# Four graph layers on one TensorE queue: another order of steps for the first and the last graphs, stored as data

## The chip, the cores and the metric

The kernel runs on one core of a Trainium2 chip. The metric is the device time of one launch in microseconds. Before the change three runs took 2764.44, 2767.73 and 2769.32 us; the median is 2767.73 us. A fourth run was taken with the hardware profiler.

## What is computed

Thirty-two graphs of 512 nodes with 256 features each pass through four layers; each layer ends in a residual and a layer norm. All is float32, and no graph needs another one.

```python
# per graph: x is 512x256, adj is 512x512
x = layernorm(x + relu(((1 + eps) * x + adj @ x) @ W1 + b1) @ W2 + b2)      # layer 0
x = layernorm(x + attention_4_heads(x, adj > 0.5, W, a_src, a_dst) + bias)  # layer 1
x = layernorm(x + attention_8_heads(x, log(adj + 1e-6), Wq, Wk, Wv) @ Wo.T + bo)  # layer 2
x = layernorm(x + softmax(((x @ W3) @ x.T) * adj) @ x)                      # layer 3
```

## The kernel before

**A list of steps, and an order.** The program does not emit its instructions graph by graph. `prepare()` and `graph(g)` register small steps in a `Plan`: each has a name, an engine, an assumed duration, the steps that it must follow, and the buffers that it takes and frees. `Plan.run` (L222) then puts all 11,118 steps of all graphs in one sequence and emits them in it; every engine executes its own part strictly in that order. I call the weight preparation set 0 and the graphs 1 to 32, so "28.d1" is the step d1 of graph 28. The order mixes the stages of several graphs: while one graph is in layer 3, the next ones are in layers 2, 1 and 0.

**How the order was found.** `Plan.order` (L134) walks forward with assumed times. Among the steps that could start soon it takes the one with the earliest due time: the graph's turn times a period of 83.965, less the longest remaining chain behind the step, plus a correction by step name, with further corrections for the first graphs, for the last graphs and for single graphs. These numbers are in one line of 78,550 characters at L1609.

**Steps that matter here** (TensorE steps, with the chain that each waits for):

- `d1` (L1175) sums the layer-1 weights. It waits for `as` (L1165), eight VectorE additions that may begin when the head's matmul `o1` (L1137) has read the weights.
- `o100` to `o111` (L1137) wait for `zm` (VectorE, L1115), these for `z` (ScalarE, L1104), and these for `Rl` (L1052), a 1 MB load that spreads a row over all partitions. It comes out of `Rt` (L1035) through a small store.
- `n0` to `n7` (L1351) wait for `m` (VectorE, L1315), these for `e` (ScalarE, L1306), these for the scores `s0` to `s7` (L1293).
- `i0`, `i1` (products recorded at L342 or L346, out iT_ps) open layer 3. In graphs 3 to 29 they wait for a turned copy of x: after `p1` come a residual and norm statistics on VectorE, one small step on GpSimd, `r3` on ScalarE, a 512 KB store to DRAM `xw3` (L710), four 128 KB loads `xl3` (L723) and two VectorE transposes `xe3` (L742).
- `la` (L821) loads a graph's adjacency in four pieces of 256 KB, `lx` (L833) its x. VectorE turns the adjacency (`at`), then `h0`, `h1` start the graph.
- `cd` and `fd` (GpSimd, L1326 and L1379) start DMAs that add one layer-2 weight tile to another.

SyncE issues `la`, `lx`, `Rl`, `xw3`, `xl3` and the outputs in one queue[...].

**Three forms of matmul.** A product is one matmul of 128 columns or, after a column-tiled step, four of 32 columns side by side (`product`, L342 and L346): such a step takes the form that TensorE is in. The scores `s` always use row tiles, `d2` tiles of 64 rows. `Plan.CHANGE` (L64) charges 0.14 to 0.22 for a change of form.

Of the kernel before, what the change touches and what calls it, by code (L numbers as in the profile page):

```python
# [16 lines left out]
P = 128  # L17
# [19 lines left out]

class Step:
# [4 lines left out]
    def __init__(self, eng, us, after, take, mode, emit):  # L43
        self.eng, self.us, self.after, self.take, self.emit = eng, us, after, take, emit
        self.mode = mode
        self.then, self.frees = [], []


class Plan:
# [51 lines left out]
    def link(self):  # L101

        self.left = [{} for _ in self.steps]
        for g in reversed(range(len(self.steps))):
            steps, left = self.steps[g], self.left[g]
            for name, s in steps.items():
                for a in s.after:
                    (self.steps[0][a[1:]] if a[0] == "^" else steps[a]).then.append((g, name))
            for k, (_, after) in enumerate(self.frees[g]):
                for a in after:  # L110
                    steps[a].frees.append(k)
        for g in reversed(range(len(self.steps))):
            steps, left = self.steps[g], self.left[g]
            for name in reversed(steps):
                s = steps[name]
                left[name] = s.us + max(
                    (self.left[h][n] + self.hop(s, self.steps[h][n]) for h, n in s.then if h - g < 2),
                    default=0.0,
                )
# [6 lines left out]
    def ready(self, g, name, ends):  # L126

        s, t = self.steps[g][name], 0.0
        for a in s.after:
            h, n = (0, a[1:]) if a[0] == "^" else (g, a)  # L130
            t = max(t, ends[h][n] + self.hop(self.steps[h][n], s))
        return t

    def order(self, period, ahead, window, stay, rush=(), moves=(), edges=(0, (), 0, (), ())):  # L134


        room = {b: [(0.0, i) for i in range(n)] for b, n in self.stock.items()}
        engine, mode, out, last = {}, "", [], 0.0
        held = [{} for _ in self.steps]
        ends = [{} for _ in self.steps]  # L140
        waits = [{n: len(s.after) for n, s in steps.items()} for steps in self.steps]
        fwaits = [[len(after) for _, after in frees] for frees in self.frees]
        ready, low, opened = {}, 0, 0
        todo = [len(steps) for steps in self.steps]
        moved = dict.fromkeys((n for steps in self.steps for n in steps), 0.0)
        turn = [max(g - 1, 0) for g in range(len(self.steps))]
        for i, early in enumerate(rush):
            turn[-1 - i] -= early
        for n, far in moves:
            moved[n] += far  # L150
        lead, tail = edges[0], len(self.steps) - edges[2]
        early, late = dict(edges[1]), dict(edges[3])
        own = {g % len(self.steps): dict(far) for g, far in edges[4]}

        def shift(g, name):
            some = early if g <= lead else late if g >= tail else {}
            return moved[name] + some.get(name, 0.0) + own.get(g, {}).get(name, 0.0)

        def near(low):
            fill, until, between, left, drain = ahead  # L160
            return fill if low < until else drain if low >= len(self.steps) - left else between

        def open_to(n):
            nonlocal opened
            while opened < min(n, len(self.steps)):
                for name in self.steps[opened]:
                    if not waits[opened][name]:
                        ready[opened, name] = self.ready(opened, name, ends)
                opened += 1

        open_to(window)
        while low < len(self.steps):
            found = []
            for (g, name), t in ready.items():
                s = self.steps[g][name]
                t = max(t, engine.get(s.eng, 0.0))
                into = self.EITHER.get(mode, "c32") if s.mode == "any" else s.mode
                change = self.CHANGE[into] if s.eng == "pe" and into != mode else 0.0
                for k, (kind, _, rest) in enumerate(s.take):
                    r, n = room[kind], sum(b[0] == kind for b in s.take[:k])  # L180
                    if len(r) <= rest + n:
                        break
                    t = max(t, r[n][0])
                else:
                    due = turn[g] * period - self.left[g][name] + shift(g, name) + stay * change
                    found.append((t, due, g, name, change))
            if not found:
                return math.inf, out
            first = min(found)[0] + near(low)
            _, t, g, name, change = min((due, t, *f) for t, due, *f in found if t <= first)  # L190
            s = self.steps[g][name]
            t += change
            if s.eng == "pe":
                mode = self.EITHER.get(mode, "c32") if s.mode == "any" else s.mode
            del ready[g, name]
            got = {}
            for kind, key, _ in s.take:
                got[key] = held[g][key] = (kind, room[kind].pop(0)[1])
            if s.eng:
                engine[s.eng] = t + s.us  # L200
            end = ends[g][name] = t + s.us
            last = max(last, end)
            out.append((g, name, mode, got))
            for h, n in s.then:
                waits[h][n] -= 1
                if not waits[h][n] and h < opened:
                    ready[h, n] = self.ready(h, n, ends)
            for k in s.frees:
                fwaits[g][k] -= 1
                if not fwaits[g][k]:  # L210
                    key, after = self.frees[g][k]
                    kind, i = held[g].pop(key)
                    free = max(ends[g][a] + self.HOP.get(self.steps[g][a].eng, 0.0) for a in after)
                    room[kind].append((free, i))
                    room[kind].sort()
            todo[g] -= 1
            while low < len(self.steps) and not todo[low]:
                low += 1
                open_to(low + window)
        return last, out  # L220

    def run(self, tries):  # L222

        self.link()
        best = min((self.order(*t)[0], t) for t in tries)
        assert best[0] < math.inf
        for g, name, self.mode, got in self.order(*best[1])[1]:
            self.slot[g].update((key, i) for key, (_, i) in got.items())
            self.steps[g][name].emit()
# [3 lines left out]
def fast_path(  # L233
# [24 lines left out]
    B, N, D = x.shape  # L258
# [27 lines left out]
    selfw = const.tile([P, P], F32, name="selfw")  # L286
# [21 lines left out]
    def blk(i):  # L308
# [3 lines left out]
    plan = Plan({  # L312
        "B": 13, "C": 12, "D": 10, "p": 8,

        "live": 6, "L0": 1, "L1": 2, "L2": 2, "L3": 1, "AT": 4, "zs": 7, "edge": 1, "tmp": 2,
    })
# [1737 lines left out]
@with_exitstack  # L2054
def four_layer_graph_kernel(ctx: ExitStack, tc: tile.TileContext, *args):
    flags = ctx.enter_context(tc.tile_pool(name="flags", bufs=1))
    beyond = flags.tile([1, 1], I32, name="beyond")
    fast_path(tc, *args, beyond)
    taken = tc.nc.values_load(beyond, min_val=0, max_val=1,
                              skip_runtime_bounds_check_because="is_lt gives 0 or 1")  # L2060
    with tc.If(taken > 0):
        general_path(tc, *args)
# [34 lines left out]
```

## Time and profile before

| | |
|---|---|
| median of three runs | 2767.73 us |
| the profiled execution | 2767.12 us, of it the span 2765.3 us |
| share of the span: TensorE, VectorE, ScalarE, GpSimd | 98%, 78%, 62%, 17% |
| mean granted TensorE clock | 0.994 |
| DMA, mean over the span | 151 GB/s |
| one graph in the middle: from 1297.05 to 1380.02, from the matmul group y_ps of one graph to that of the next | 82.97 us |
| the last group of matmuls of the last graph ends at | 2752.6 us |

Thirty-two times 82.97 us is 2655.0 us; the other 110.3 us of the span are the preparation, the filling of the pipeline and its emptying. In the groups below, "idle before" a matmul is time in which TensorE had nothing that it could do, and the arrow names what ended it. A matmul's end is modelled in the profile, so some waiting may lie inside the busy time too.

### The profile page before, as it was taken

Reading aid. Unit: us, or ns where it says so; the run is one execution under the profiler, and the core shown is the slowest. Engines: PE = TensorE matmul, PEld = TensorE weight load, DVE = VectorE, ACT = ScalarE, POOL = GpSimd, SP = SyncE. Lnnn points to the kernel's source line nnn. Section 1 sums busy time; section 2 is a strip of 40 time slices with the busy share of each in tenths; the row PEclk is TensorE's granted clock in tenths of the full one; section 3 lists DMA queues with packets and bytes.
Section 4 is the critical chain, followed back from the end, with each engine's and each line's share of the span. In section 5 each row is a group of like instructions: output and inputs, shape, how many; then the busy total and the mean of one; then the engine's idle time right before and its main releaser. Section 6 shows DMA issues by size and latency. Waiting matters only on the chain.

```text
span 2765.3 us, 68089 instructions
## 1 busy us (share of the span) xinstructions
PE 2716.7 (98%) x28680; PEld 1317.9 (48%) x28680; DVE 2158.8 (78%) x4257; ACT 1720.4 (62%) x3320; POOL 474.8 (17%) x526
## 2 busy tenths in 40 slices
PE   8999999999999999999999999999999999899998
PEld 6544444444445444445444445444444443444443
DVE  3887778877879877879877879877878877578975
ACT  3676665666666666666666666666665665556853
POOL 1111211121111121111121111121111111111110
PEclk9999999999999999999999999999999999999999
DMA  8487787778888879888878888888896988736760
GB/s 167 80 168 150 148 168 147 160 160 163 158 163 151 171 157 169 162 156 153 174 162 160 149 171 151 171 157 169 155 163 135 182 168 163 156 73 146 155 131 17
DMA packets 476735, 418.76 MB, mean 151 GB/s; under 512 B 377788, under 2 KB 431496, under 8 KB 444552
## 3 DMA queue, kind: packets, MB, share of 16 engines
q0 software_dynamic: 45568, 277.89, 53.1%
q1 hardware_dynamic: 429872, 136.18, 24.2%
q8 instruction: 227, 3.72, 0.5%
q14 instruction: 84, 0.69, 0.1%
q10 hardware_dynamic: 984, 0.28, 0.0%
HBM read 155.53 MB, written 31.24 MB: 68 GB/s over the span
## 4 chain that ended last, share of the span: by engine, by line
PE 86%; DVE 6%; DMA 3%; issue 2%; ACT 1%; POOL 0%; SPq 0%; DVEq 0%; POOLq 0%; ACTq 0%
PE s L1293 8%; PE o_ps L1351 7%; PE v_ps L346 7%; PE y_ps L342 7%; PE o_ps L346 6%; PE o_ps L1137 6%; PE hT_ps L346 6%; PE s L346 5%; PE h1T_ps L346 4%; PE o2p_ps L346 3%; PE iT_ps L342 3%; PE s L342 3%; PE h1T_ps L342 3%; PE kT_ps L342 2%; DVE z L1115 2%; PE qT_ps L346 2%
## 5 line engine op out<-in xcount | busy, mean ns | idle before, releaser
L1315 DVE SCALAR_TENSOR_TENSOR z<-AT,z 128x1024 f32<-128x1024 f32 x512 | 612.6, 1214 | 108.2 <-ACT z L1306 107.0
L1306 ACT ACTIVATE z<-s 128x512 f32<-128x512 f32 x1024 | 541.4, 608 | 109.2 <-PE s L1293 103.4
L1104 ACT ACTIVATE z<-R_bc,nT,S 128x512 f32<-128x512 f32 x512 | 373.4, 807 | 72.0 <-DMA z<-z 58.2
L684 ACT ACTIVATE x<-x,shift,rstd 128x256 f32<-128x256 f32 x508 | 273.9, 593 | 179.6 <-DVE shift L669 174.8
L1115 DVE SCALAR_TENSOR_TENSOR z<-z,T,edge 128x512 f32<-128x512 f32 x512 | 346.5, 742 | 5.8 <-ACT z L1104 5.8
L1326 POOL DMA_DIRECT2D z<-z x186 | 174.4, 942 | 868.4 <-PE o_ps L1351 445.3
L661 POOL TENSOR_TENSOR rstd<-ve,nhalf 128x4 f32<-128x4 f32 (+1 forms) x131 | 169.0, 1339 | 854.8 <-DVE ve L655 846.6
L1293 PE MATMUL s<-qT,kT 32*128 32x512 f32 x2048 | 278.4, 626 | 0.4 <-ACT kT L1264 0.4
L1351 PE MATMUL o_ps<-z,v 128*32 128x512 f32 x2048 | 254.9, 599 | 2.6 <-DVE z L1315 1.4
L1539 DVE TENSOR_TENSOR z<-s,AT 128x512 f32<-128x512 f32 x128 | 88.4, 690 | 214.9 <-PE s L342 110.1
L1137 PE MATMUL o_ps<-z,v 128*32 128x512 f32 x2048 | 233.8, 595 | 2.5 <-DVE z L1115 2.5
L1165 DVE TENSOR_TENSOR z<-z 128x1024 f32<-128x1024 f32 (+1 forms) x256 | 229.5, 949 | 0.7 <-PE o_ps L1137 0.7
L638 DVE BATCH_NORM_STATS2 st<-x 128x6 f32<-128x256 f32 x508 | 212.7, 419 | 10.6
L346 PE MATMUL o_ps<-x,z 128*32 128x257 f32 x3520 | 202.4, 380 | 0.0
L346 PE MATMUL hT_ps<-AT,x 128*32 128x256 f32 (+2 forms) x2640 | 185.5, 380 | 0.0
L342 PE MATMUL y_ps<-w_sb,h1T 128*128 128x256 f32 x832 | 184.4, 379 | 0.0
L342 PEld LDWEIGHTS y_ps<-w_sb,h1T 128*128 128x128 f32 x832 | 156.1, 190 | 21.5 <-issue 1.0
L1293 PEld LDWEIGHTS s<-qT,kT 32*128 32x128 f32 x2048 | 96.7, 184 | 143.5 <-issue 63.6
L346 PEld LDWEIGHTS o_ps<-x,z 128*32 128x32 f32 x3520 | 114.8, 110 | 83.8 <-issue 6.9
L346 PE MATMUL h1T_ps<-hT,w_sb 128*32 128x512 f32 x1296 | 147.9, 595 | 0.0
L625 POOL DMA_DIRECT2D x<-biases x96 | 103.8, 1081 | 237.0 <-issue 67.7
L346 PE MATMUL s<-iT,xT 128*32 128x512 f32 x1232 | 139.4, 592 | 0.1
(188 smaller groups left out, 3858.7 us busy)
## 6 DMA issues: line engine op xcount, KB each, us to landing
z<-z POOLq DMA_DIRECT2D x186, 1024.0 KB, 8.7
x<-biases POOLq DMA_DIRECT2D x96, 512.0 KB, 9.6
R_bc<-R_dram SPq DMA_DIRECT2D x32, 1024.0 KB
Ar<-in_adj_dram SPq DMA_DIRECT2D x124, 256.0 KB
z<-z POOLq DMA_DIRECT2D x62, 512.0 KB, 7.7
x<-in_x_dram SPq DMA_DIRECT2D x32, 512.0 KB
out_dram<-x SPq DMA_DIRECT2D x31, 512.0 KB
x_dram<-x SPq DMA_DIRECT2D x27, 512.0 KB
```

Source lines behind the costliest of these rows:

```text
L342: nc.tensor.matmul(out, lhsT, rhs, start=start, stop=stop)
L346: nc.tensor.matmul(out[part], lhsT[:, part], rhs, start=start, stop=stop)
L638: nc.vector.bn_stats(t[f"st{n}"][:, c, :], t["xo" if n == 4 else "x"][:, c, :D])
L684: nc.scalar.activation(t[into][:, c, :D] if into else xn, xn, AF.Identity, bias=t[f"shift{n}"][:, c : c + 1], scale=t[f"rstd{n}"][:, c : c ...
L1104: nc.scalar.activation(t[f"e{h}"][:, c, :], t["Rbc"][:, h, :], AF.Relu, bias=t["nT"][:, h, c : c + 1], scale=t["S"][:, h, c : c + 1],)
L1115: nc.vector.scalar_tensor_tensor(z, z, t["T"][:, h, c : c + 1], t["edge"][:, c, :], op0=ALU.add, op1=ALU.mult)
L1137: nc.tensor.matmul(po[32 * q : 32 * q + 32, :], t["v"][:, c, hp * P + 32 * q : hp * P + 32 * q + 32], t[f"e{2*hp+q//2}"][:, c, :], start=( ...
L1165: nc.vector.tensor_add(z[:, :m, :], z[:, :m, :], z[:, m : 2 * m, :])
L1293: nc.tensor.matmul(pk, t["k"][hs, o, blk(c)], t["q"][hs, o, :], start=True, stop=True)
L1306: nc.scalar.activation(t[f"E{k}"][:, j, :], t[f"ps{k}{j}"], AF.Exp, scale=QSCALE)
L1315: nc.vector.scalar_tensor_tensor(z, t["AT"][:, c, None, :].to_broadcast([P, 2, N]), ADJ_EPS, z, op0=ALU.add, op1=ALU.mult,)
L1351: nc.tensor.matmul(t[f"n{o}"][32 * j : 32 * j + 32, :], t["v2"][:, c, o * P + F2 * j : o * P + F2 * (j + 1)], t[f"E{k}"][:, j, :], start=( ...
```

## The change

The search is gone from the kernel. The order is a constant string: two bytes for each step, namely how far its graph lies ahead of the oldest unfinished one, and its place among that graph's steps that are left. `sequence` unpacks it, and `run` walks it once with the old assumed durations, only to decide which buffer of a kind each step gets.

```diff
+ORDER = (
+    'c-rk;*^=bA4Fo}ux~uw{@%D}<?En8tBNL#idcEV=h<$Q|)H78&cp-6+Dx@SLCAZiUY;jy-Po=2(Kg9|4bIQx=--7b0qlKcZttiWH'
...
+)
-    def order(self, period, ahead, window, stay, rush=(), moves=(), edges=(0, (), 0, (), ())):
...
-            first = min(found)[0] + near(low)
-            _, t, g, name, change = min((due, t, *f) for t, due, *f in found if t <= first)
...
+    def sequence(self, text):
+        data = zlib.decompress(base64.b85decode(text))
+        left, low = [list(steps) for steps in self.steps], 0
+        for ahead, place in zip(data[: len(data) // 2], data[len(data) // 2 :]):
+            g = low + ahead
+            yield g, left[g].pop(place)
+            while low < len(left) and not left[low]:
+                low += 1
+        assert low == len(left)
-    def run(self, tries):
+    def run(self, text):
         self.link()
...
+        for g, name in self.sequence(text):
...
+            s.emit()
...
     with tc.manual_schedule():
...
+        plan.run(ORDER)
```

No step is added, removed or altered: both programs have the same 11,118 steps with the same instructions but for the form that a product takes. Of TensorE's 2,077 steps, the 1,317 from t1 of graph 4 to h1 of graph 28 stand at the same places in both; about 360 before and 400 after them stand in another order. On the other engines the same holds: VectorE keeps 2,076 of 3,242 steps in one unchanged stretch, ScalarE 2,025 of 3,193, GpSimd 331 of 509, SyncE 309 of 467.

TensorE's order near the end, as an example (a step's form: ' column tiles, r row tiles, R rows by 64):

```
before: 28.o100' 29.h1' 28.o101' 28.o110' 28.o111' 27.s6r 28.yt0 28.yt1 28.yt2 28.yt3 28.d1' 29.f0'
after:  28.o100' 28.o101' 28.o110' 29.f0' 29.f1' 29.f2' 28.o111' 29.f3' 28.d1' 27.n6' 28.dt 28.yt0

before: 27.p1' 29.y0' 29.y1' 28.s5r 30.h0' 28.s6r 30.h1' 28.n5' 28.s7r 28.n6' 29.xt10 29.xt11
        30.f0 30.f1 28.n7' 29.v10' 29.v11' 29.v12' 29.v13' 27.i0'
after:  27.p1' 28.s6r 28.n3' 28.n4' 29.y1' 28.n5' 28.s7r 30.h0' 30.h1' 28.n6' 30.f0' 29.xt10 29.xt11
        30.f1 29.v10 29.v11 29.v12 29.v13 30.f2 29.Rt 30.f3 27.i0
```

and SyncE's there:

```
before: 30.la0..3 30.lx 25.out 31.la0 31.lx 31.la1..3 27.xw3 26.out 27.xl30..33 29.Rs 29.xs 29.hsb 29.Rl
        32.la0 32.lx 32.la1..3 28.xw3 28.xl30..33 27.out
after:  25.out 30.la0..3 30.lx 31.la0..2 27.xw3 27.xl30..33 31.la3 31.lx 29.xs 29.Rs 29.Rl 29.hsb 26.out
        28.xw3 32.la0..2 28.xl30..33 32.la3 30.Rs 30.Rl 32.lx
```

## The prediction

> **What bounds the kernel now.** I read first the page's shares and its 40 slices.
>
> ```profile
> PE 2716.7 (98%) x28680; PEld 1317.9 (48%) x28680; DVE 2158.8 (78%) x4257; ACT 1720.4 (62%) x3320; POOL 474.8 (17%) x526
> ...
> PE   8999999999999999999999999999999999899998
> ```
>
> TensorE (PE) is the bound: full in all slices but the first, one late one and the last. An order without fewer matmuls can win only what TensorE does not use. So I cut the span into stretches of 83 us, about one graph each, by the windows view (columns: stretch, its length, busy time of PE, PEld, DVE, ACT and POOL, granted clock, DMA share, GB/s).
>
> ```profile
> 249.00:332.00 83.00, 81.19 (x773) 38.35 (x769) 59.70 (x103) 51.82 (x106) 15.22 (x17) 1.00 0.77 142
> ...
> 498.00:581.00 83.00, 83.00 (x925) 40.15 (x921) 67.77 (x134) 53.40 (x105) 14.89 (x16) 1.00 0.80 155
> ...
> 2240.00:2323.00 83.00, 79.55 (x804) 36.16 (x797) 63.55 (x122) 50.57 (x97) 13.70 (x15) 0.98 0.82 162
> 2323.00:2406.00 83.00, 74.94 (x849) 35.52 (x848) 46.89 (x92) 39.36 (x80) 12.57 (x15) 0.96 0.89 176
> ...
> 2489.00:2572.00 83.00, 79.42 (x836) 39.26 (x830) 72.27 (x148) 55.95 (x104) 11.72 (x13) 0.98 0.62 134
> ```
>
> The middle has no hole, and there both programs have one order: nothing is to be won or lost there. The holes lie before 500 us and after 2100 us, where the order changes. The wait view, cut to these two parts, names them (engine, line, what it waited for: total, times, longest): first from 2100 us on, then from 12 to 500 us.
>
> ```profile
> PE iT_ps L346 <- DVE xT L742: 8.0, 1, 8.0
> PE d_ps L1175 <- DVE z L1165: 3.4, 2, 3.1
> ...
> PE o_ps L1137 <- DVE z L1115: 2.5, 2, 1.5
> PE o_ps L1351 <- DVE z L1315: 1.4, 1, 1.4
> ```
> ```profile
> PE d_ps L1175 <- DVE z L1165: 2.3, 2, 1.7
> PE gg L546 <- DVE gm L540: 2.0, 1, 2.0
> PE o_ps L1351 <- DVE y L1210: 1.3, 1, 1.3
> ```
>
> With the smaller ones the waits sum to 8.1 us in the first part and 20.0 in the last, leaving out the final check's. A wait costs more than itself: behind some the granted clock drops.
>
> ```profile
> 2386.90:2390.30 3.40, 3.34 (x17) 0.68 (x18) 0.60 (x2) 0.64 (x4) 0.00 (x0) 0.54 0.95 193
> ...
> 2513.00:2516.40 3.40, 3.40 (x34) 1.53 (x28) 3.39 (x6) 3.40 (x7) 0.93 (x1) 0.52 0.78 140
> ...
> 2646.00:2649.40 3.40, 3.40 (x16) 0.70 (x12) 2.60 (x7) 1.40 (x3) 2.75 (x3) 0.50 1.15 231
> ```
>
> In 3.4 us at half clock half the work is done: 1.7 us lost. It happens five times (near 212, 2294, 2383, 2513, 2646), once with only 3.0 us of it under matmuls: about 8.3 us. Here a rule speaks against this reckoning. The Trainium skill, "TensorE: Matmul & The Clock Gate", section "Why this matters for your kernels", has the clock fall only after a gap of some 3 us. By it only the 8.0 us wait would cost, 1.5 us. The trace has the drop behind 1.26 us (at 211.69), 1.38 and 1.49 us, yet none behind 1.70 us at 259.59. I follow the trace: a removed wait of over 1.2 us takes 1.7 us along where the trace shows it.
>
> **The change, part by part.** For every TensorE step I looked up its latest TensorE ancestor and summed the matmul work that stands between the two in each order (h 3.5, f 1.77, y 3.46, o1 1.74, i, p, w, q and k 1.72, v 0.89, n and s 0.86, d1 1.0: intervals between starts in the middle of the trace). That cover must outlast the other engines' chain.
>
> *d1 of graph 28* waited 3.05 us, to 2294.89. Its eight additions cost 4 times 1.22 and 4 times 0.68, 7.6 us of VectorE; the cover from o110 was 3.7 us. After: 8.8. The wait goes, with the clock: 4.7 us. *d1 of graphs 4 and 5* waited 1.70 and 0.64; cover 7.0 becomes 18.3 and 9.6: 2.3 us. Graphs 27, 29 and 30 get 7.0, a length at which 0.1 to 1.7 us were waited: 0.5 each goes into the new stalls below.
>
> *i0 of graph 27* is the largest: 7.96 and 1.5. Its cover hardly moves, 27.8 to 27.7. What decides is the chain behind 27.p1 (end at 2350.8), which the chain view shows (start, us, what):
>
> ```profile
> 2361.71 0.57 SPq L723
> 2362.33 1.42 SPq L723
> 2363.80 4.56 SPq L723
> 2368.40 5.02 DMA xL<-x_dram
> ...
> 2374.54 11.47 issue
> 2386.10 0.72 DVE xT L742
> 2386.96 3.41 PE iT_ps L346 x16
> ```
>
> The turned loads started 10.9 us after p1; VectorE then waited until 2386.0. In the semaphore records 15 of 16 parts of the last load are in by 2379.1 and the last one at 2385.9. Before them in the queue stood 27.xw3 and 26.out, 512 KB each, and behind 2326 us five loads for graph 31. After: 26.out stands behind, and 31.la3 and 31.lx too; 31.la0 to la2 stand directly ahead. They need graph 30's adjacency turned; after the change that lies about 15 us of matmul work before 27.p1, so they are likely issued before xw3 is ready. Without 26.out (2.4 us between the landings of xw3 and it) and without a late part: 28.3 - 2.4 + 1.6 for xe3 = 27.5 us against 27.7: no wait. If parts come late again: 7 us. In graph 28 the whole chain took 29.2 us, a wait of 1.5. I take 3.5 with its clock, so 6 of 9.5 are won; the ends are 0 and 9.5.
>
> *o100, o101 of graph 30* waited 1.49 and 1.00, with a drop. Cover from Rt 24.2 and 29.4 becomes 26.9 and 32.1, 2.7 more than before, and the waits sum to 2.5. Taken 3.5 of 4.2. *n4 of graph 2* (1.26 and a drop): cover 3.5 becomes 21.1, 3.0 us. *dt of 32 and n4 of 31* (0.49, 1.38, a drop): n6 no longer follows so closely, n4 has 13.8 for 12.0 and dt 1.3 for 0.1, but VectorE is behind there with the additions of graph 32 in both orders; taken 2.0 of 3.6. *k0* followed its copy directly in graphs 2, 5, 27 and nearly in 6, and waited 0.24, 0.24, 0.24, 0.66; s0 of graph 2 0.45: cover grows in all of them, 1.8.
>
> *The start.* SyncE issues x second, and the third and fourth adjacency pieces wait for other landings; both orders need all 1.5 MB and the fourth piece before h0, and that one waits for the load of a0 in both. On ScalarE three small bias loads now stand between the first and the second copy of the adjacency. In the trace their last one was held until 8.1 us by another load. After, it waits for the third adjacency piece, which lands earlier (issued without a wait). I take nothing, with 2 us either way. gg of the preparation (2.0) has less cover, 0.4 for 1.4, but VectorE no longer has graph 2's adjacency between: 1.0 won. Against that f0 of graph 1 follows its copies directly (0.3), and Rt of graph 1 stands 0.3 behind v13, where 1.3 of cover and 0.2 of waiting were seen: 1.2 lost. Sum -0.5.
>
> *Changes of form.* Two s steps in a row take 1.93 us, one alone 1.07: entering row form costs 0.21, and by a fit over 1,200 groups entering the full form 0.06 and column form from the full one 0.02. Counted over both orders, entries to row form fall from 187 to 179, to the full form from 135 to 120, to column form by 18: 1.7 + 0.9 + 0.4 = 3.0 us. The planner's 0.14 to 0.22 for each would say 7; the trace decides.
>
> *The end.* Behind the last matmul (2752.6) the same steps follow. SyncE now issues the outputs of 31, 30 and 29 together just before those of 32: 1.5 MB in the 10.5 us before 32's first, 143 GB/s, with the DMA otherwise idle (the last slice has 17 GB/s). Nothing, at most 2 us.
>
> Sum: 4.7 + 2.3 + 6 + 3.5 + 3.0 + 2.0 + 1.8 - 0.5 + 3.0 = 25.8. Against it I set 2.8 for stalls that the old trace cannot show: the three d1 at 7.0 (1.5) and three s0 at 1.1 us behind their copies, where 1.9 was seen without a wait (1.3). Net 23: the profiled execution's 2767.1 becomes 2744.1; its time lies 0.6 below the median of the runs, so from 2767.7 I say 2744.7.
>
> **Rivals.** *The waits move (0.22).* VectorE is busy 72 of 83 us near 2500; a gap that one step leaves is taken by the next. If 27.i0 keeps its 9.5 us and the three d1 wait 1.7 each with one drop, 25.8 - 6 - 5.3 - 2 leaves 12: 2756. For it: i0's cover has not grown. Against it: the other covers grow well beyond the waits. *All goes (0.15).* Every wait of 28.1 us, the drops of 8.3 and the 3.0 would give 2728 at most; more likely 2733. *No change (0.10):* new waits of some 20 us, as much as the old ones. *Slower (0.08).* SyncE's queue in order: 32.la0 to la2 now stand between 28.xw3 and 28.xl3, 31.la0 to la2 before 27.xw3, 32.la3 before 30.Rl. In the old trace SyncE needed from 2326.06 to 2342.94, 17 us, for five such loads, held by earlier landings. Put before 28.xl3, that moves its end from 29.2 to 41 us against a cover of 33.5: 7.5 and 1.7. One place does not decide; from about three such places on, at 9 us each, the gain of 23 is gone, and four give 2780. Against it: in the window from 2406 the DMA share is 0.38 only. That the order is not what the change says is no case: the placement is counted from both programs.
>
> **How the numbers follow.** The main case has 0.45 and reaches from 2738 to 2751. With the moved waits and most of the best case, 2731 to 2761 holds 8 in 10. A measurement of this kernel tells some 0.2%, 5.5 us: faster (below 2762.2) are the main case, the best and the moved waits, 0.82; same 0.10; slower 0.08.
>
> **What would show it.** d_ps should wait under 3 us in all instead of 5.8, and the clock should drop at most twice behind the start; o_ps at L1137 and L1351 together under 2; iT_ps under 4. The middle should keep 82.97 us a graph. Wrong would be: a first d1 or o100 with a long wait for a DMA, 28.i0 waiting for xT, or h0 of graph 1 starting later than 13 us.

## The result, and the profile after

The changed kernel takes 2757.79 us (median of 10 runs, 2754.79 to 2766.32) beside 2765.69 us (10 runs) for the kernel before: a ratio of 0.9975, 95% interval 0.9965 to 0.9985. So 7.9 us are won where 23 were forecast, a third. The profiled execution of the changed kernel took 2757.91 us, its span 2756.2, which is 9.1 us under the span before.

On the page TensorE is busy 2699.6 us (2716.7 before), and its slices have two dents near the end in place of one:

```profile
PE   8999999999999999999999999999999999898998
```

The windows view over the last three of the stretches shown of before (columns as there: the first number behind the length is TensorE's busy time) shows where:

```profile
2240.00:2323.00 83.00, 82.62 (x942) 37.60 (x934) 65.26 (x127) 54.69 (x105) 12.68 (x13) 1.00 0.80 160
2323.00:2406.00 83.00, 70.07 (x881) 33.68 (x881) 44.06 (x91) 37.23 (x73) 13.58 (x14) 0.92 0.82 158
2489.00:2572.00 83.00, 75.13 (x810) 36.50 (x806) 67.75 (x141) 54.22 (x101) 12.48 (x13) 0.96 0.57 122
```

From 2240 to 2323 us 3.1 us were won. From 2323 to 2406 TensorE is busy 70.1 us where it was 74.9, and from 2489 to 2572 75.1 for 79.4. The wait view says what took the place of the old waits: first from 2100 us on, then from 12 to 510 us.

```profile
PE iT_ps L327 <- DVE xT L727: 13.3, 2, 12.9
PE hT_ps L331 <- DVE z L1100: 5.9, 1, 5.9
```
```profile
PE s L1278 <- ACT kT L1249: 6.5, 1, 6.5
PE hT_ps L327 <- DVE ATd L844: 2.2, 1, 2.2
```

The reader should look for what is missing. The long waits of d_ps on VectorE (3.4 and 2.3 us before) have no row, and those of o_ps on VectorE (2.5, 1.4 and 1.3) have none either. In their place stand four others: i0 of graph 27 (12.9 us, 8.0 before), s0 of graph 2 (6.5), h0 of graph 32 (5.9) and h0 of graph 1 (2.2). The granted clock falls around the three long ones:

```profile
178.70:188.90 10.20, 5.94 (x28) 1.50 (x32) 7.13 (x10) 7.37 (x14) 0.80 (x1) 0.50 0.74 131
2373.40:2387.10 13.70, 4.14 (x5) 1.85 (x6) 1.49 (x3) 0.32 (x1) 1.79 (x3) 0.50 1.18 193
2496.30:2503.10 6.80, 5.13 (x66) 3.56 (x70) 6.51 (x12) 6.80 (x14) 0.73 (x1) 0.50 0.87 178
```

The second number is TensorE's busy time at half clock: 15.2 us, so about 7.6 us of work are lost, as much as before (8.3).

### The profile page after: what moved, and what is told of

The parts are those of the page before. It is cut to its first block, busy times and chain, and to the rows that moved or that the text cites. A ratio compares the mean times of both kernels' runs of the same rounds, so it can differ in the third digit from the quotient of the medians.

```text
span 2756.2 us, 68553 instructions
## 1 busy us (share of the span) xinstructions
PE 2699.6 (98%) x28884; PEld 1309.0 (47%) x28884; DVE 2162.4 (78%) x4257; ACT 1716.5 (62%) x3320; POOL 480.4 (17%) x526
## 4 chain that ended last, share of the span: by engine, by line
PE 81%; DMA 4%; DVE 3%; issue 1%; ACT 1%; SPq 1%; POOL 0%; DVEq 0%; POOLq 0%; ACTq 0%
PE s L1278 8%; PE o_ps L1336 7%; PE o_ps L331 7%; PE o_ps L1122 6%; PE v_ps L331 6%; PE hT_ps L331 6%; PE y_ps L327 5%; PE h1T_ps L331 4%; PE s L331 4%; PE o2p_ps L331 4%; PE s L327 3%; PE iT_ps L327 3%; DMA z<-z 2%; PE qT_ps L327 2%; PE kT_ps L331 2%; PE kT_ps L327 2%
## 5 line engine op out<-in xcount | busy, mean ns | idle before, releaser
L1278 PE MATMUL s<-qT,kT 32*128 32x512 f32 x2048 | 272.8, 626 | 6.5 <-ACT kT L1249 6.5
L1336 PE MATMUL o_ps<-z,v 128*32 128x512 f32 x2048 | 249.7, 596 | 0.0
L1150 DVE TENSOR_TENSOR z<-z 128x512 f32<-128x512 f32 (+1 forms) x256 | 229.5, 950 | 6.0 <-PE o_ps L1122 5.4
L1122 PE MATMUL o_ps<-z,v 128*32 128x512 f32 x2048 | 229.4, 593 | 1.1 <-ACT z L1291 1.1
L331 PE MATMUL o_ps<-x,z 128*32 128x257 f32 x3744 | 214.3, 380 | 0.0
L331 PE MATMUL hT_ps<-AT,x 128*32 128x384 f32 (+2 forms) x2592 | 181.5, 383 | 0.0
L331 PEld LDWEIGHTS o_ps<-x,z 128*32 128x32 f32 x3744 | 120.9, 110 | 87.8 <-issue 5.7
L1122 PEld LDWEIGHTS o_ps<-z,v 128*32 128x32 f32 x2048 | 65.3, 110 | 149.3 <-issue 125.3
```

The lines of the kernel that those rows point to most:

```text
L331: nc.tensor.matmul(out[part], lhsT[:, part], rhs, start=start, stop=stop)
L1122: nc.tensor.matmul(po[32 * q : 32 * q + 32, :], t["v"][:, c, hp * P + 32 * q : hp * P + 32 * q + 32], t[f"e{2*hp+q//2}"][:, c, :], start=( ...
L1150: nc.vector.tensor_add(z[:, :m, :], z[:, :m, :], z[:, m : 2 * m, :])
L1278: nc.tensor.matmul(pk, t["k"][hs, o, blk(c)], t["q"][hs, o, :], start=True, stop=True)
L1336: nc.tensor.matmul(t[f"n{o}"][32 * j : 32 * j + 32, :], t["v2"][:, c, o * P + F2 * j : o * P + F2 * (j + 1)], t[f"E{k}"][:, j, :], start=( ...
```

## What the four new waits wait for

*i0 of graph 27.* The chain view of the changed kernel (start, us, what), to be held against the one of before:

```profile
2348.82 12.68 DMA x_dram<-x
...
2363.77 6.96 SPq L708
...
2370.78 11.29 DMA xL<-x_dram
...
2382.96 5.73 PE iT_ps L327 x8
```

SyncE's timeline of before, at the same store and loads:

```profile
2358.33 0.56 SPq L710 DMA_DIRECT2D x_dram<-x  x1
...
2361.70 8.18 SPq L723 DMA_DIRECT2D xL<-x_dram  x4
```

The store 27.xw3 takes 12.7 us to land; before the change the loads behind it could be issued 3.4 us after it. Behind it the four loads take another 20 us. The store is also issued 9.5 us earlier than before (2348.82 for 2358.33), since 27.p1 ends 8.6 us earlier (about 2342.2 for 2350.8); yet i0 starts only 4.0 us earlier (2382.96 for 2386.96).

*s0 of graph 2.* ScalarE's timeline (start, busy, step; in brackets the idle time before it and its releaser):

```profile
176.01 0.56 ACT L1249 COPY qT<-qT_ps 128x512 f32<-128x512 f32 x1
180.92 1.52 ACT L1089 ACTIVATE z<-R_bc,nT,S 128x512 f32<-128x512 f32 x2 [4.35 <-DMA z<-z]
182.35 0.56 ACT L1249 COPY kT<-kT_ps 128x512 f32<-128x512 f32 x1
```

The copy 2.ke0, whose product ended at 170.5, stands behind 3.z30. That step waits 4.35 us until a GpSimd addition has left the buffer it writes. s0 starts at 182.96.

*h0 of graph 32.* Its x is loaded last in SyncE's queue, behind 30.Rl. It is issued at 2483.1, when 28.t3 leaves a buffer for it, and lands 14.8 us later; before the change it was issued at 2397.

*h0 of graph 1* starts at 13.95 us, 11.21 before. The eps load, which VectorE's first step waits for, lands at 10.05 (4.7 before), and on ScalarE the second copy of the adjacency stands behind the bias loads, which are issued at 9.86 to 12.26.

## Experiments

Each kernel runs all of the work. A line such as ("a b", "before", "c") takes the steps a and b out of the unpacked sequence and puts them directly before c; the queues change only there, and the buffers that the walk gives out follow. In the first two runs the string was packed anew from both orders; they are cut at a point where both orders have the same 5000 steps behind them. As the runs of a kernel scatter by some 5 to 11 us, the ratios to the kernel before, taken in the same session, are compared; the changed kernel's is 0.9975.

**The first graphs alone, the last graphs alone.**

```diff
-order = new
+order = new[:5000] + old[5000:]    # first_graphs
+order = old[:5000] + new[5000:]    # last_graphs
```

> The new order for the first 5000 steps, the old order for the rest (both have the same 5000 steps behind them at that point, and the order of the middle graphs is the same in both). By TensorE's lost time in the two profiles the new order is 3.0 us ahead at 500 us (33.3 against 30.3), form changes included only in part. My theory, that every stretch won on VectorE is half given back in queues of ScalarE and of transfers: about 3 to 4.5 us under the kernel before, near 2762. Rival, that the whole gain is made in the last graphs: within 1 us of before, near 2765.

> The old order for the first 5000 steps, the new order for the rest. By the lost time, 41.5 us behind 500 us before and 38.2 after, and some 2 us of form changes: my theory says 4 to 6 us under the kernel before, near 2760.5, so that this and the other half add up to the 7.9 us measured. Rival, whole gain in the last graphs: 8 us, near 2757.5. A third, that the two halves disturb each other: they do not add up to 7.9 within 2 us.

Measured: 0.9994 (0.9985 to 1.0003) for the first graphs alone and 0.9975 (0.9965 to 0.9984) for the last alone; medians 2763.16 and 2759.08 beside 2765.11. The rival fits best: what the runs can show to be won is won in the last graphs. The first part's 3.0 us by TensorE's lost time are within the interval's lower end, 4.1 us, but not shown. In this profile Rt of graph 7 waited 3.98 us, 1.08 in the changed kernel's (see at8_behind).

**s0 of graph 2: the copy ahead of the waiting step.**

```diff
+    ("2.qe0 2.ke0", "before", "3.z20"),
+    ("3.z30 3.z31 3.zm30 3.z32", "behind", "3.oe0"),
```

> The new order, with the copies 2.qe0 and 2.ke0 ahead of 3.z20 on ScalarE and 3.z30, 3.z31, 3.z32 behind 3.oe0. My theory: s0 of graph 2 waited 6.46 us for 2.ke0, which stood behind 3.z30, which waited 4.35 us for a transfer into its buffer; with the copy ahead s0 starts 6 us earlier, the clock does not fall for 10 us, and the time is 7 to 10 us under the changed kernel, near 2749. Rival, the buffer is late whatever stands where: the wait goes on to the next o or s of graph 3, and under 3 us are won, 2755 to 2758.

Measured: 0.9967 (0.9955 to 0.9979), 2756.70 us. In the trace the wait and the fall of the clock are gone: s0 starts at 176.38. Of these 6.6 us, 3.9 are left at k0 of graph 3 (245.88 for 249.76), because o110 of graph 3 now waits 2.46 us for the late buffer, as the rival had it (under 3 us won; by the ratios 2 us, which these runs can't tell from none). The lead is 3.8 us at h0 of graph 27 and 1.6 at i0 of graph 27. So the copy's place was the cause of this stall, but less reaches the end than the stall was long.

**i0 of graph 27: the loads ahead of it.**

```diff
+    ("31.la0i 31.la1i 31.la2i", "before", "31.la3i"),
```

> The new order, with the three adjacency loads 31.la0 to 31.la2 on SyncE behind 27.xl33 in place of ahead of 27.xw3. My theory: i0 of graph 27 waited 12.93 us because its turned copy stood behind these loads; the wait falls under 6 us (it was 7.96 before the change), and the time is 5 to 10 us under the changed kernel, near 2750. Rival, the 16 engines are full there with GpSimd's additions into memory: xw3 and xl land as late, the wait stays over 11 us and under 2 us are won; a second rival, the loads come too late for h0 of graph 31, which then waits 5 us or more.

Measured: 0.9974 (0.9965 to 0.9984), and i0 waits 13.01 us. My theory fell: 27.xw3 took as long (12.74 us) without the three loads directly ahead of it. Their place in SyncE's queue isn't the cause. The wait view named the copy, the chain named the store; neither names what the store shares the DMA engines with. GpSimd's rows do: the additions of 1 MB 28.cd5 and 28.cd2 were issued 2.4 and 0.9 us before the store. In the old order one addition was under way, and it landed 1.9 us after the store was issued. GpSimd's timeline, first of before (store at 2358.33), then of after (store at 2348.82):

```profile
2343.30 0.86 POOL L1326 DMA_DIRECT2D z<-z  x1 [8.55 <-DVE rd_all L1565]
2351.53 0.86 POOL L1326 DMA_DIRECT2D z<-z  x1 [7.36 <-issue]
```
```profile
2346.46 0.90 POOL L1311 DMA_DIRECT2D z<-z  x1
2347.96 0.86 POOL L1311 DMA_DIRECT2D z<-z  x1 [0.60 <-DMA z<-z]
```

**The start; the load of graph 32; the additions.** Three repairs and all of them together.

```diff
+    ("0.ld_eps", "before", "0.ld_a"), ("1.lxi", "behind", "1.la1i"),           # start_order
+    ("0.ld_bias 0.bias.q 0.b1.q", "behind", "1.ate3"),
+    ("31.xt10 31.xt11", "behind", "28.t3"), ("32.lxi", "before", "30.Rsi"),     # lx32_ahead
+    ("28.cd5 28.cd2", "behind", "29.dev1.0"),                                   # cd_behind
```

> The new order, with the load of eps first on ScalarE, the three bias loads behind the copy 1.ate3, and 1.lx behind 1.la1 on SyncE, as the old order has the first two of these. My theory: h0 of graph 1 stood at 13.95 us against 11.21 because eps landed at 10.05 (VectorE's selfw waits for it) and ate1 stood behind the bias loads; now at0 starts near 4.5, h0 near 11.3, and the time is 2 to 3 us under the changed kernel. Rival: h0 is early, but f0 waits for W1 all the same (it stood at 22.73 and 23.31), and the gain is under 1 us.

Measured: 0.9971 (0.9959 to 0.9983). In the trace h0 starts at 12.10 and f0 at 21.10 (23.31); the 2.2 us stay to the end (span 2753.8). The runs can't tell 2 us from none.

> The new order, with 32.lx ahead of 30.Rs on SyncE (it then takes the buffer that 30.xT1 leaves at 2472 us) and 31.xt10, 31.xt11 behind 28.t3 on TensorE (they take the one that 28.iT leaves at 2483). My theory: h0 of graph 32 waited 5.92 us because its load was issued at 2483 for want of a buffer and landed 14.8 us later; issued 11 us earlier it lands before 2492, the wait and the fall of the clock to half for 6.8 us go, and the time is 6 to 9 us under the changed kernel. Rival: the wait for a buffer only moves, and 31.xt10 or 31.v10 stands as long: under 2 us.

Measured: 0.9957 (0.9944 to 0.9970), 2754.41 us. The load was issued at 2471.8, 11 us earlier, yet h0 still waited 4.85 us. Here is why, on ScalarE's timeline of this run:

```profile
2492.88 1.52 ACT L1107 ACTIVATE z<-R_bc,nT,S 128x512 f32<-128x512 f32 x2 [5.00 <-DMA R_bc<-R_dram]
2494.30 0.58 ACT L1309 ACTIVATE z<-s 128x512 f32<-128x512 f32 x1
```

The last row is 29.e73. It empties the bank that h0 of graph 32 writes, and VectorE's 32.atd stands behind its reader; it is held by 30.z00, which waits for the row of graph 30 to land. The rival was right that another wait lay just under this one.

> The new order, with GpSimd's additions into memory 28.cd5 and 28.cd2 behind 29.dev1 (6 us later), so that they are not under way while 27.xw3 is written. The run with 31.la0 to la2 behind left i0 of graph 27 waiting 13.0 us, so those loads are not the cause. New theory: 27.xw3 took 12.7 us to land (3.4 before the change) because two additions of 1 MB shared the 16 engines with it; now it lands in under 6 us, the wait of i0 falls to 5 to 8 us, and the time is 5 to 9 us under the changed kernel. Rival: xw3 is early but the four reads behind it meet the same additions, xe30 comes as late, and i0 still waits over 11 us.

Measured: 0.9955 (0.9942 to 0.9968), 2753.17 us. The chain view of this run:

```profile
2349.51 3.22 DMA x_dram<-x
...
2354.87 24.09 DMA xL<-x_dram
...
2379.86 4.49 PE iT_ps L344 x6
```

The store lands in 3.2 us when the two additions come behind it (they are issued from 2354.48 on): that cause of the slow store is shown. The last load, though, now takes 24.1 us where it took 11.3, so i0 waits 9.14 us. Both readings hold in part.

> The new order with all of these: start, 32.lx ahead, 28.cd5 and 28.cd2 behind, the copies 2.qe0, 2.ke0, 2.qe1, 2.ke1 ahead of 3.z30 on ScalarE with 2.v21 and 2.v22 ahead of 3.o110 on TensorE, and 8.at0 to at3 behind 7.ed1 on VectorE (the wait of Rt of graph 7 was 0.5 to 4 us from run to run, because 7.ab stood behind 8.at0, which waits for a load). My theory: 2 + 6 + 7 + 6 + 2 = 23 us, less what turns up elsewhere: 2735 to 2742. Rival, that the stalls are set by the 16 engines' sum of work and come back in other places: 2750 or more.

Measured: 0.9928 (0.9915 to 0.9941), 2745.35 us, 20.3 under the kernel before. Waits left: 7.73 us at i0 of graph 27, 4.33 at h0 of graph 32, 2.38 at o110 of graph 3.

**h0 of graph 32: two holds.**

```diff
+    ("29.e73", "before", "30.z00"),                                             # e73_ahead
+    ("29.e73", "before", "30.z00"),                       # e73_lx32: added to those of lx32_ahead
```

> The new order, with the copy 29.e73 ahead of 30.z00 on ScalarE. With 32.lx early, h0 of graph 32 still waited 4.85 us: its bank is left by 29.e73, which stood behind 30.z00 and 30.z01, and 30.z00 waited 5.0 us for the broadcast row 30.Rl to land. First theory, both the load and the bank hold h0 (32.lx lands at 2497.8, h0 starts at 2497.97): with the bank alone free at 2488 nothing is won, h0 waits over 5 us, and the time is within 2 us of the changed kernel's 2757.8. Second theory, only the bank held it: h0 starts by 2493 and 5 us or more are won.

> The new order, with 29.e73 ahead of 30.z00 and 32.lx early as in lx32_ahead. First theory (two things held h0 of graph 32 within 1 us of each other): now its wait falls under 1 us, the clock does not fall there, and the time is 6 to 9 us under the changed kernel, near 2750. Rival: a third thing holds it (32.atd on VectorE behind 29.m71): it still waits over 3 us, and under 4 us are won.

Measured: the bank alone 0.9992 (0.9983 to 1.0001), slower than the changed kernel: h0 waits 10.7 us, since 32.lx takes 19.5 us to land and not 14.8. With the earlier copy GpSimd starts the addition 29.cd7 8.4 us behind that load instead of 13.1; that this is what holds the load is read from one profile, not isolated. Both together 0.9949 (0.9935 to 0.9962), 2750.58 us: the wait of h0 and the fall of the clock are gone; 1.7 us at Rt of graph 31 are left. Against the changed kernel's 2497.97, h0 of graph 32 starts at 2496.84 with the load alone and at 2493.24 with both. By the ratios the load alone wins 5 us, the bank alone loses 5, and both win 7, each with some 4 us of uncertainty: two holds of nearly the same length, and only their sum shows.

**i0 of graph 27, followed to the end.**

```diff
+    ("28.cd5 28.cd2 28.cq5", "behind", "28.cd7"),                               # cd7_ahead
+    ("31.lxi 31.lx.q 31.lx", "behind", "29.hsbi"),
+    ("27.one", "before", "28.fd0"),                                             # one_ahead, added to these
```

> The new order, with 28.cd5 and 28.cd2 behind 28.cd7 on GpSimd (5 us later than in cd_behind) and the load 31.lx behind 29.hsb on SyncE. In cd_behind 27.xw3 landed in 3.3 us, but the four reads issued 3 to 5 us behind it landed 21 us later, beside three additions of 1 MB and 31.lx, with the 16 engines full. Theory, the reads need a stretch of their own: now they land before the additions begin, i0 of graph 27 waits under 3 us (12.93 in the changed kernel, 9.14 in cd_behind), and the time is 9 to 13 us under the changed kernel, near 2747. Rival, a delay of the additions is paid back at the end of graph 28 (its d2) or at h0 of graph 31: under 5 us.

> cd7_ahead with the fill 27.one ahead of 28.fd0 on GpSimd. In cd7_ahead i0 of graph 27 no longer waited, but w0 of graph 27 waited 9.75 us for 27.one, which is ready when r30 is read and stood behind 28.fd1, which waits for the additions to land. Theory: the wait of w0 goes too, and the time is 9 to 14 us under the changed kernel, near 2746. Rival, the additions' delay is paid at d2 of graph 28, which is the next step on TensorE: it waits 8 us or more, and under 4 us are won.

Measured: 0.9973 (0.9964 to 0.9982) and 0.9984 (0.9975 to 0.9993): nothing is won. The wait views from 2360 to 2410 us, first of cd7_ahead, then of one_ahead:

```profile
PE o_ps L349 <- POOL x L1499: 9.8, 1, 9.8
```
```profile
PE d_ps L1402 <- DMA z<-z: 12.6, 2, 10.8
```

With the additions later i0 waits no more (from 12.9 us to none), and w0 of graph 27 waits 9.8 us for a fill of GpSimd behind them. With that ahead too, d2 of graph 28 waits 12.6 us, in two waits, for the additions themselves. h0 of graph 31 starts at 2413.1, 2413.8 and 2414.8 us in the three kernels. Here the wait only changes its name: the additions of graph 28 end no earlier, and TensorE's order has nothing else at these places. Another order might have; none was tried.

**Does one VectorE wait bring what the sum took for it?** The old order with one change:

```diff
+    ("25.st41 25.wx2 25.st42 25.wx3", "behind", "28.as01"),
```

> The old order with one change: 25.st41, 25.wx2, 25.st42 and 25.wx3 behind 28.as01 on VectorE (2.2 us of work put behind the step that d1 of graph 28 waits for). The sum took 4.7 us for the end of this stall of 3.05 us with its fall of the clock. Theory, a VectorE stall taken away brings its own length and the clock's: the wait falls to about 0.8 us, the clock stays, and the time is 2 to 4 us under the kernel before, near 2762.5. Rival, the time comes back at i0 of graph 27, whose transfers do not depend on TensorE: under 1 us, i0 waits 10 us in place of 8.

Measured: 0.9996 (0.9987 to 1.0005), 2764.07 beside 2764.69. The wait of d1 falls from 3.05 to 1.34 us; the clock falls all the same. The windows view of this run:

```profile
2294.20:2297.60 3.40, 3.40 (x31) 1.10 (x20) 3.26 (x9) 0.37 (x1) 0.28 (x1) 0.51 0.57 88
```

d1 starts 1.43 us earlier than in the profile of before; of this lead 0.25 us are left at h0 of graph 30, 64 us later, 0.40 at i0 of graph 27 (which waits 7.82 us, 7.96 before), and 0.3 in the span. By the ratio 1.1 us are won, anything from 3.6 won to 1.4 lost, so the runs' time does not rule out the first theory. In this pair of profiles neither theory has it: the clock falls all the same, and most of the lead is gone before the transfers come in. Which steps take it, I can't say from one profile.

**All repairs again.** The second uses cd7_ahead's places and 29.e73 ahead; the third adds 27.one and the steps of graph 31 ahead; the fourth goes back to cd_behind's places.

```diff
+    ("30.z00 30.z01 30.z02 30.z03 30.z10 30.z11", "behind", "31.v13"),          # third and fourth
+    ("31.ve10 31.ve11 31.ve12 31.ve13", "before", "30.z00"),
+    ("31.ab", "behind", "31.ve13"), ("31.R", "behind", "30.z01"),
```

> All of all_repairs, with cd7_ahead's places in place of cd_behind's, and 29.e73 ahead of 30.z00. It stood at 2745.4 with waits of 7.73 us at i0 of graph 27 and 4.33 at h0 of graph 32, each with a fall of the clock. Theory: 5 + 2 us and 4 + 2 us go, 2731 to 2735. Rival, other waits take their place: 2740 or more.

> all_repairs_2 with 27.one ahead of 28.fd0, and with the copies 31.ve10 to ve13, 31.ab and 31.R ahead on ScalarE and VectorE of the work of graph 30 that waits for its broadcast row (Rt of graph 31 waited 2.81 us). Theory: 9.6 us of w0, 2.8 of Rt and some 5 us of half clock go from 2745: 2728 to 2733. Rival, the additions' delay comes out at d2 of graph 28: 2740 or more.

> all_repairs (additions 28.cd5, 28.cd2 6 us later only, 31.lx and 27.one where the new order has them), with 29.e73, 31.ve10 to ve13, 31.ab and 31.R ahead on ScalarE and VectorE as in all_repairs_3. Theory: graphs 27 and 28 are bound by their stream of additions, which all_repairs_2 and 3 began later and so lengthened (h0 of graph 31 at 2409.9 and 2413.0 against 2402.2); with it early and the 4.33 us of h0 of graph 32 gone the time is 2738 to 2741. Rival, the wait of graph 32 only moves to the next transfer: 2744 or more.

Measured: 0.9926 (0.9913 to 0.9940), 0.9928 (0.9915 to 0.9942) and 0.9903 (0.9888 to 0.9918); medians 2745.16, 2746.76 and 2739.30 us. The second and third win the 4 to 5 us of graph 32 and lose as much by the later additions; the fourth keeps both gains. It is the fastest kernel here, 27 us under the kernel before (2766.38 in its session) and, by the ratios, 20 under the changed one. Its repairs were tried only together. Its wait view from 2100 us on:

```profile
PE iT_ps L358 <- DVE xT L758: 10.0, 2, 9.6
PE ok_ps L1634 <- DVE okr L1632: 3.2, 1, 3.2
```

One long wait is left besides the final check's, the one that transfers set; no other row is over 0.7 us.

**The scatter.**

```diff
+    ("8.at0 8.at1 8.at2 8.at3", "behind", "7.ed1"),
```

> The new order, with 8.at0 to 8.at3 behind 7.ed1 on VectorE and nothing else. The wait of Rt of graph 7 was 1.08 us in the profile of the changed kernel, 0.5 to 1.5 in seven of the other profiles that have these places and 3.5 to 4.0, with a fall of the clock, in four. Theory: it goes, the time is 2 to 3 us under the changed kernel's 2757.8 and its runs lie closer together (a spread of 6 us or less, 11.5 for the changed kernel). Rival: under 1 us, spread as before.

Six of the other profiles with these places, not seven, lie between 0.5 and 1.5 us. Measured: 0.9968 (0.9956 to 0.9980), 2757.00 us. The wait of Rt of graph 7 is gone, here and in the four kernels with all repairs. Five of the six runs lie between 2756.0 and 2758.9, the sixth at 2762.5, and its profile has a wait of 3.11 us elsewhere, near 2122. That the scatter comes from this wait is likely, and not shown.

## Why the prediction was wrong

The signs it named fell as follows.

- **d1 and n4, the VectorE waits: right about the waits.** d1 of graphs 4, 5 and 28, o100 and o101 of graph 30, n4 of graphs 2 and 31 and dt of 32 wait 0.3 us or less, and their falls of the clock are gone. The three d1 and three s0 for which 2.8 us were set aside cost nothing that has a row. What they were worth is another matter: "4.7 us" for d1 of graph 28 counted the wait as if TensorE's time up to the end depended on it. d1_alone took 1.7 us from this wait and left the fall of the clock; the span of its one profile is 0.3 us shorter, and its runs show no gain clear of their scatter.
- **i0 of graph 27: the failed step.** The sum said "Without 26.out ... and without a late part: ... no wait" and took +6. It has become 5.0 us longer, with 2.1 us lost at half clock for 1.5: a miss of 11.6 us, the largest of all. The step priced the store and the loads by what stands before them in SyncE's queue. The store's time is set by GpSimd's additions beside it: it took 3.4 us before, 12.7 after and 3.2 in cd_behind. It came to meet them because it was issued 9.5 us earlier, 0.9 us behind an addition instead of 6.8; the prediction kept the chain behind p1 at its old length. What slowed the loads in cd_behind (24.1 us) is not isolated: with the additions later still (cd7_ahead) i0 has no such wait, but 31.lx was moved there too. That transfers started by different engines interleave on the same 16 engines is stated in the Trainium skill ("DMA: Bandwidth & Descriptors", section "Issuing engines are not separate DMA queues"); what it costs, the 3.2 and 12.7 us show. The rival "slower" had the right place and the wrong cause: it blamed the loads 31.la, and la31_behind, where i0 waits 13.0 us with these loads behind, shows that they are not it.
- **32.lx: not looked at.** The change puts it behind 30.Rl, 86 us later than before, and in the same stroke 29.e73 behind 30.z00. The wait is 5.9 us, with 5.1 us of work at half clock, 2.6 lost: 8.5 us that the sum does not have. With the load alone put right h0 still waits 4.85 us.
- **n4 of graph 2 and s0:** +3.0 and part of 1.8 were won there, and s0 of graph 2 lost 6.5 and 3.0 by 2.ke0 behind 3.z30. The cover was reckoned between TensorE's steps; ScalarE's queue between them was not read.
- **The start:** -0.5 with 2 either way. h0 is 2.7 us late, past the 13 us named as a sign; f0, which has to wait for its weights, is 0.6 late. Inside the bound, but "nothing" for the bias loads was too little for h0.
- **Changes of form, the end and the middle.** The 3.0 us of form changes are a count from the two orders times a fit; no run measures them by themselves. The end and the middle are right: from i0 of graph 32 to the end of the span 30.8 us before, 31.0 after; eight graphs of the middle 663.7 and 663.9 us.

**The ledger.** From each TensorE step's start I take off the matmul work ahead of it in its order; what grows is lost time. Behind the first step (it starts 1.2 us later) it splits so, in us:

| | before | after |
|---|---|---|
| waits between steps, as the wait view has them | 31.2 | 39.0 |
| work lost at half clock | 8.1 | 7.6 |
| what is left over, taken to lie inside steps | 30.9 | 16.0 |

With 3.0 us less of form changes the sum is 1.2 + 7.8 - 0.5 - 14.9 - 3.0 = -9.4, and the spans differ by 9.1. So the waits that the prediction was about got longer, not shorter, and what was won lies where it did not look: in the rest. Of the 14.9 us, 7.7 are between 60 and 500 us, 2.3 between 2200 and 2300 and 2.5 between 2500 and 2700. A matmul's end is modelled, so a step that stops between two of its matmuls counts as busy; its weight loads tell. The timeline of weight loads in the kernel before, at s7 of graph 4, which lost 1.8 us without a row in the wait view:

```profile
378.82 0.29 PEld L1293 LDWEIGHTS s<-qT,kT 32*128 32x128 f32 x2 [0.18 <-ACT z L1306]
379.79 0.44 PEld L1293 LDWEIGHTS s<-qT,kT 32*128 32x128 f32 x4 [0.68 <-ACT z L1306]
380.99 2.10 PEld L346 LDWEIGHTS y_ps<-w_sb,h1T 128*32 128x32 f32 x44 [0.76 <-DVE x L1219]
```

The scores go bank by bank as ScalarE empties them. The new order leaves more work between such steps, which the prediction credited only to the few of them that had a row. That this is the cause of all 14.9 us is inferred from where they lie; no run here isolates it.

The number nearest to the result is the rival's "the waits move", 2756. That is in good part luck: it let i0 keep its 9.5 us and the three d1 wait, while i0 grew by 5.6 us with its clock, two copies on ScalarE and a load took over, none of the three d1 waited, and the 14.9 us of the rest are in no term of it.

## What to carry to other kernels

When an order is changed on a tuned kernel, read every in-order queue, not only that of the bound engine: for each step that waits for a transfer, ask which short step now stands behind it (2.ke0, 29.e73, 27.one and 7.ab here), and move those ahead. Price a transfer by what shares the DMA engines in that stretch, and expect that an engine that is made earlier starts its transfers earlier, into others (27.xw3, 9.5 us earlier). A wait that only changes its name when its cause is moved (i0, then w0, then d2) points to a stretch that is bound by something else; look for that before moving another step of the waiting engine.

## What the runs showed of the hardware

- A 512 KB store took 3.2 to 3.4 us to land with at most one addition ending beside it, 12.7 us beside two additions of 1 MB; the last of four 128 KB loads took up to 24.1 us (cd_behind). In the changed kernel, from 2350 to 2390 us the DMA engines moved 188 to 194 GB/s at a busy share of 0.98 to 1.08.
- With a copy of 0.6 us put ahead (e73_ahead), an addition started 4.7 us sooner behind a load of another graph, and that load took 4.7 us longer to land (19.5 for 14.8). One profile; the link is argued.
- In the windows view the clock fell to half for 3.4 us behind a wait of 1.34 us (d1_alone), and for 10.2 and 13.7 us around waits of 6.5 and 12.9 us, in multiples of about 3.4 us; behind the wait of 1.33 us at k0 of graph 3 it did not fall (1.00 from 249.70 to 253.10). So the length of one wait does not decide it here; what does, these runs don't show.
